# A transposed image in DRAM, laid out by row, place and tile column instead of by place, row and tile column

## The chip, the cores and the metric

The kernel runs on one core of one Trainium2 chip. The metric is the device time of one execution in microseconds. The kernel before takes 2478.38 us, the median of 3 runs (2473.84 to 2490.16). The execution that the profile shows has a span of 2488.3 us.

## The reference

The input x has 8 images of 256 channels and 56 x 56 pixels, in float32. Two layers follow each other, each with a residual.

```python
# layer 0: an involution: a 7x7 kernel per pixel and per group of 16 channels
def _L0_conv_ref(x, w_reduce, b_reduce, w_span, b_span):
    ker = jnp.einsum('bchw,oc->bohw', x, w_reduce) + b_reduce[None, :, None, None]
    ker = jnp.einsum('bchw,oc->bohw', ker, w_span) + b_span[None, :, None, None]
    ker = ker.reshape(B, G, 1, K * K, H, W)
    xp = jnp.pad(x, ((0, 0), (0, 0), (PAD, PAD), (PAD, PAD)))
    patches = jnp.stack([xp[:, :, i:i + H, j:j + W] for i in range(K) for j in range(K)], axis=2)
    patches = patches.reshape(B, G, C // G, K * K, H, W)
    return (ker * patches).sum(axis=3).reshape(B, C, H, W)

x = x + _L0_conv_ref(_gn(x), ...)
# layer 1: group norm, then twice: 3x3 convolution with ternary weights, batch norm over all 8
# images, relu (the second adds the output of the first before its relu)
x = x + _L1_conv_ref(_gn(x), ...)
```

Here G = 16, K = 7, and `_gn` is a group norm with 32 groups. Each image's group norm needs the whole image, and each batch norm needs all images.

## The kernel before

The program has four stages. **Start:** the first image is loaded, its norm is computed, its transposed copy is written to DRAM, and both convolution weights are made ternary (`quantize`). **Involution:** 8 images, each as 4 "quarters". A quarter is 64 channels, and the upper and the lower half of the image lie in the two halves of the 128 partitions (`h * CH`), so one half image is 28 rows. **Two convolutions**, with a pass over all images each. **The end:** norms, residual and the output. The change touches the first two stages alone.

The involution is done as matrix products over tiles of `PY` x `PX` = 3 x 8 pixels. Such a tile needs a patch of `QY` x `QX` = 9 x 14 = 126 input pixels. A half image has `TY` = 10 rows of tiles and `TX` = 7 tile columns. To use the 126 pixels of a patch as the contraction, the normalised image must lie with pixels in partitions and channels in the free dimension. So it is transposed and kept in DRAM in `xt_d`, twice (even and odd images), per quarter. A "place" is a column of the patch, 0 to 13. Each tile column has its own 14 places, so neighbouring tile columns hold 6 of the places double.

- `prep(b)` writes the transposed copy of image b. It works on strips of `SR` = 14 rows. For one strip, GpSimd normalises it into `xn` (one buffer, line 559). In a later step of the order, TensorE transposes `xn` in 8 pieces, one for each x within a tile (line 567), into a PSUM tile of the pool `ps_p` (3 buffers, shared with `generate`, `reduce` and `quantize`), ScalarE copies it to `stg` (line 570), and tasks are left for SyncE to store it: the strip at its own places, the same again for the columns that are places of the tile before and of the tile after, and the 3 rows that the other half of the image needs as its border. This makes 6 stores a strip, in pieces of 512 bytes and, for the border, 256 bytes. `transfer()` issues one task in each row step.
- `load_q` (line 599) loads the 126 patch rows of one row of tiles, 126 partitions with 3584 bytes each, 4 row steps ahead (`NQB`).
- `generate` makes the matrices of the next quarter in 14 units of 24 or 32 matmuls (line 629) whose results VectorE (638) and ScalarE (633) take out of PSUM with the bias added.
- `apply_row` does the 56 matmuls of one row of tiles (line 662); `pick_out` takes the wanted blocks by ScalarE (674) and VectorE (675), and GpSimd adds them to the image (678).
- `reduce` makes the next image's reduced channels (line 526), during the third quarter.

The main loop walks through 40 row steps for each image, r = 0 to 39, 10 in each quarter. `pin` makes the order of the text the order on every engine. In one row step stand: one store of the finished quarter or one load of the next image (`X_AT` says at which r), one `transfer()`, `apply_row`, one `load_q`, statistics, `pick_out`, up to two units of `generate` (`PER_ROW`), and one half step of `prep` where r is in `STRIP_AT`. A half step is either the GpSimd operation of a strip or its transposes with what follows, so a strip takes two half steps. The next image's strips begin at r = 23 and end at r = 6 of the next image itself.

In the start the first image's strips are all done in a row, with no `pin`: `prep(0)` stands in the text before `quantize(w1)`, whose sum over partitions is a matmul (line 203) that VectorE needs for the mean (line 205). All units of the first quarter and `quantize(w2)` follow, and the buffers of `load_q` lie where the memory of `quantize` was.

Of the kernel before, what the change touches and what calls it, by code (L numbers as in the profile page):

```python
# [7 lines left out]
F32 = mybir.dt.float32  # L8
F32R = mybir.dt.float32r
AF = mybir.ActivationFunctionType  # L10
ALU = mybir.AluOpType
# [4 lines left out]
P = 128  # L16
# [24 lines left out]
LEAD = (PX - 1) * QY + PY - 1  # L41
# [4 lines left out]
KX = TX + 1  # L46
HQ = TY * PY + K - 1
EX = HQ * KX
SR = HH // 2
NSP = SR * KX  # L50

# [24 lines left out]
def involution_tri_block_kernel(  # L76
# [17 lines left out]
    xt_d = [[dram.tile([QX * EX, P], F32, tag=f"xtd{i}_{c}", name=f"xtd{i}_{c}")  # L94
# [338 lines left out]
    with ExitStack() as ph1:  # L433
# [70 lines left out]
        xn = fixed([P, PX, SR, KX], "xn")  # L504
        nc.gpsimd.memset(xn, 0.0)
        zero = xn.rearrange("p j r k -> p (j r k)")

        for d in (d for ds in xt_d for d in ds):
            for r0, n in ((0, 5), (PAD + HH, 8)):
                e = P * 5  # L510
                nc.sync.dma_start(
                    bass.AP(d[:].tensor, d[:].offset + r0 * KX * P, [[EX * P, QX], [e, n], [1, e]]),
                    zero[:QX * n, :e])
# [27 lines left out]
        PLACES = ((PX - PAD, PX, 1), (0, PX, 0), (0, QX - PX - PAD, -1))  # L541

        def prep(b):
# [3 lines left out]
            for c in range(NCQ):  # L547
                d = xt_d[b % 2][c][:]

                def store(src, j0, j1, shift, row, o, d=d):  # L550

                    x0 = PAD + j0 - PX * shift
                    n, w = src.shape[0], src.shape[2]
                    nc.sync.dma_start(
                        bass.AP(d.tensor, d.offset + (x0 * EX + row * KX + shift) * P + o,
                                [[P, n], [EX * P, j1 - j0], [1, w]]), src[:, j0:j1])

                for s in range(2):
                    nc.gpsimd.tensor_scalar(  # L559
                        xn[:, :, :, :TX].rearrange("p j r k -> p r k j"),  # L560
                        xs[b, c][:, s * SR * W:(s + 1) * SR * W].rearrange(
                            "p (r k j) -> p r k j", k=TX, j=PX),
                        prm[b][:, c, 0:1], prm[b][:, c, 1:2], ALU.mult, ALU.add)
                    yield
                    pt = ps_flat(f"pt_{b}_{c}_{s}")
                    for j in range(PX):
                        nc.tensor.transpose(pt[:NSP, j * P:(j + 1) * P],  # L567
                                            xn[:, j].rearrange("p r k -> p (r k)"), ident_sb)
                    stg = work.tile([P, PX, P], F32, tag="stg", name=f"stg_{b}_{c}_{s}")
                    nc.scalar.copy(stg[:NSP].rearrange("p j c -> p (j c)"), pt[:NSP])  # L570
                    before, own, after = PLACES

                    e = PAD * KX
                    border = (stg[:e, :, CH:], PAD + HH, 0) if s == 0 else \
                        (stg[NSP - e:NSP, :, :CH], 0, CH)
                    whole = (stg[:NSP], PAD + s * SR, 0)
                    for part in (((whole, own),), ((whole, before), (whole, after)),
                                 ((border, own), (border, before), (border, after))):
                        def run(part=part, store=store):
                            for (src, row, o), pl in part:  # L580
                                store(src, *pl, row, o)
                        tasks.append(run)
                    yield
# [9 lines left out]
        def load_q(b, c, ty):  # L593
# [3 lines left out]
            src = bass.AP(d.tensor, d.offset + PY * ty * KX * P,  # L597
                          [[EX * P, QX], [KX * P, QY], [1, TX * P]])
# [9 lines left out]
        def generate(b, c, a):  # L608
# [4 lines left out]
            for u in range(NU):  # L613
# [6 lines left out]
                for j in order:  # L620
                    py, px = (p0 + j) // PX, (p0 + j) % PX
                    o = LEAD - px * QY - py
# [134 lines left out]
        X_AT = (0, 1, 4, 5, 6, 7, 8, 9)  # L757
# [150 lines left out]
```

## Time and profile before

| | us |
|---|---|
| median of 3 runs | 2478.38 |
| span of the profile | 2488.3 |
| TensorE matmul busy | 1785.1 (72%) |
| TensorE weight load busy | 1672.5 (67%) |
| VectorE busy | 1665.6 (67%) |
| ScalarE busy | 1126.5 (45%) |
| GpSimd busy | 286.9 (12%) |

The stages can be told by the slices of the profile: about 191 us for the start, then 1154 us for the involution (about 147 us for each image), then about 895 us for the two convolutions and 248 us for the end. In the involution the DMA engines are busy for 79% of the time and move 220 GB/s; in the convolutions they are busy for about a third of it. The busy share of an engine says little here by itself, as every stage has another limit; what ends the idle time of TensorE in the involution is what has to be read.

### The profile page before, as it was taken

To read this page: it belongs to the slowest core of one execution; us is meant where nothing else is said; L and a number is where in the kernel's file an instruction comes from. 1 tells how busy PE (TensorE), PEld (TensorE's weight loads), DVE (VectorE), ACT (ScalarE), POOL (GpSimd) and SP (SyncE) were. 2 spreads that over 40 slices of the span, in tenths; PEclk is the share of its full clock that TensorE was granted. 3 is DMA by queue.
4 is the path that set the end of the run, shared out by engine and by line. 5 is a ranking of instruction groups with operands and counts; after the bars stand their busy time and mean duration, and the time that the engine had idled before them with its cause. 6 is when DMAs were issued, how large, how long until landed. Compare 5 with 4: busy or idle time off the path is not lost.

```text
span 2488.3 us, 68764 instructions
## 1 busy us (share of the span) xinstructions
PE 1785.1 (72%) x30120; PEld 1672.5 (67%) x30120; DVE 1665.6 (67%) x2554; ACT 1126.5 (45%) x2020; POOL 286.9 (12%) x427
## 2 busy tenths in 40 slices
PE   1416877878786887868775999999499999990000
PEld 1306766767675776767665999999499999990000
DVE  4475656464555646556556999999599999974444
ACT  0202433434343343434433667667356767754443
POOL 0101221212122121222211000000000000000000
PEclk9657988989899898989997999999799999995555
DMA  6538696887869687796866233232423323329998
GB/s 170 162 124 220 190 250 196 235 236 204 241 181 255 194 243 202 213 249 171 247 182 223 106 129 135 106 132 106 181 81 132 133 106 127 138 73 424 429 428 377
DMA packets 216199, 493.15 MB, mean 198 GB/s; under 512 B 38446, under 2 KB 139180, under 8 KB 207196
## 3 DMA queue, kind: packets, MB, share of 16 engines
q1 hardware_dynamic: 209584, 447.66, 56.6%
q10 hardware_dynamic: 6316, 41.09, 4.1%
q8 instruction: 237, 3.88, 0.6%
q14 instruction: 62, 0.51, 0.1%
HBM read 315.88 MB, written 172.81 MB: 196 GB/s over the span
## 4 chain that ended last, share of the span: by engine, by line
PE 64%; DMA 14%; issue 10%; DVE 7%; POOL 2%; ACT 2%; ACTq 0%; SPq 0%; POOLq 0%; DVEq 0%
PE c L386 34%; PE pg L629 15%; PE pa L662 8%; DMA y1f<-y1d 4%; PE pt L567 3%; PE pk L526 3%; DMA out_y<-x1f 3%; DMA q<-xtd 2%; POOL xn L559 2%; DVE a L638 2%; DMA w_w<-in_w 1%; DVE x1f L848 1%; DMA x1f<-x1d 1%; DMA y2f<-y2d 1%; ACT a L633 1%
## 5 line engine op out<-in xcount | busy, mean ns | idle before, releaser
L386 PE MATMUL c<-pl,wq 128*128 128x392 f32 x4608 | 857.1, 348 | 50.6 <-ACT pl L292 32.5
L386 PEld LDWEIGHTS c<-pl,wq 128*128 128x128 f32 x4608 | 855.2, 189 | 52.3 <-ACT pl L292 33.2
L638 DVE TENSOR_TENSOR a<-pg,bt 126x756 f32<-126x756 f32 (+3 forms) x640 | 393.5, 656 | 288.5 <-ACT a L633 255.9
L629 PE MATMUL pg<-kr,wl 64*126 64x140 f32 (+1 forms) x6144 | 493.5, 308 | 64.7 <-issue 39.6
L629 PEld LDWEIGHTS pg<-kr,wl 64*126 64x126 f32 x6144 | 428.5, 210 | 86.8 <-issue 61.5
L662 PE MATMUL pa<-a,q 126*32 126x48 f32 x17920 | 294.9, 215 | 220.5 <-issue 140.8
L662 PEld LDWEIGHTS pa<-a,q 126*32 126x32 f32 x17920 | 240.8, 117 | 279.1 <-issue 224.6
L633 ACT ACTIVATE a<-pg,bt 126x126 f32<-126x126 f32 x768 | 243.6, 475 | 235.6 <-PE pg L629 235.4
L674 ACT ACTIVATE inv<-pa,half_sb 128x168 f32<-128x168 f32 x320 | 125.8, 393 | 428.4 <-PE pa L662 418.7
L675 DVE SCALAR_TENSOR_TENSOR inv<-pa,half_sb,inv 128x168 f32<-128x168 f32 x320 | 117.9, 368 | 231.1 <-ACT inv L674 230.5
L678 POOL TENSOR_TENSOR x<-x,inv 128x168 f32<-128x168 f32 x320 | 165.8, 518 | 909.5 <-DVE inv L675 874.5
L292 ACT CAST pl<-r 128x812 fp32r<-128x812 f32 x192 | 162.4, 867 | 153.4 <-DVE r L287 136.4
L349 ACT ACTIVATE dummy<-y,nc 128x1568 f32<-128x1568 f32 x128 | 205.4, 1605 | 15.6 <-DVE y L372 14.3
L293 DVE TENSOR_TENSOR pl<-r,pl 128x812 fp32r<-128x812 f32 x192 | 186.5, 997 | 30.6 <-ACT pl L292 29.7
L137 DVE BATCH_NORM_STATS2 st<-x 128x6 f32<-128x392 f32 x256 | 137.6, 555 | 16.9 <-DMA x<-in_x 16.3
L829 ACT ACTIVATE xp<-raw,bi_bn,sc_bn 128x392 f32<-128x392 f32 (+1 forms) x128 | 84.8, 720 | 71.7 <-DVE a L287 57.1
L559 POOL TENSOR_SCALAR xn<-x,gn 128x784 f32<-128x784 f32 x64 | 108.6, 1696 | 28.1 <-PE pt L567 21.3
L819 ACT ACTIVATE xp<-raw,gn 128x392 f32<-128x392 f32 (+1 forms) x128 | 85.2, 721 | 56.7 <-DVE a L287 50.9
L567 PE MATMUL pt<-ident_sb,xn 128*112 128x128 f32 x512 | 79.9, 306 | 29.1 <-POOL xn L559 23.4
L273 POOL MEMSET xp<- 128x116 f32 x32 | 6.3, 197 | 818.5 <-DVE a L287 818.3
L846 DVE SCALAR_TENSOR_TENSOR y1f<-y2f,sc_bn,y1f 128x3136 f32<-128x3136 f32 x16 | 55.8, 3485 | 63.9 <-DMA y2f<-y2d 63.9
L570 ACT COPY stg<-pt 112x1024 f32<-112x1024 f32 x64 | 65.5, 1023 | 71.7 <-PE pt L567 46.4
(127 smaller groups left out, 1362.6 us busy)
## 6 DMA issues: line engine op xcount, KB each, us to landing
q<-xtd SPq DMA_DIRECT2D x320, 441.0 KB
xtd<-stg SPq DMA_DIRECT2D x64, 448.0 KB
raw<-x1d SPq DMA_DIRECT2D x32, 812.0 KB
raw<-y1d SPq DMA_DIRECT2D x32, 812.0 KB
x<-in_x SPq DMA_DIRECT2D x64, 392.0 KB
x1d<-x SPq DMA_DIRECT2D x64, 392.0 KB
y1d<-y SPq DMA_DIRECT2D x32, 784.0 KB
y2d<-y SPq DMA_DIRECT2D x32, 784.0 KB
```

Source lines behind the costliest of these rows:

```text
L137: nc.vector.bn_stats(st[:, j, :], xt[:, j * NC:(j + 1) * NC])
L292: nc.scalar.copy(hi, r)
L293: nc.vector.tensor_tensor(lo, r, hi.bitcast(F32), ALU.subtract)
L349: nc.scalar.activation(dummy, y[:, to], f, bias=shift[:, to:to + 1], accum_out=stats[:, to, j, n:n + 1])
L386: nc.tensor.matmul(ps[:, to, :NM], wq[:, k, t, dx, to * P:(to + 1) * P], part[:, t, :, dx:dx + W], start=(c == 0), stop=(c == last))
L559: nc.gpsimd.tensor_scalar(xn[:, :, :, :TX].rearrange("p j r k -> p r k j"), xs[b, c][:, s * SR * W:(s + 1) * SR * W].rearrange("p (r k j) ...
L567: nc.tensor.transpose(pt[:NSP, j * P:(j + 1) * P], xn[:, j].rearrange("p r k -> p (r k)"), ident_sb)
L629: nc.tensor.matmul(dst, wl[rows, c, gp, o:o + NQ], kr[py][rows, px, :], start=True, stop=True)
L633: nc.scalar.activation(whole[:, g0 + i, p0 + j], ps[:NQ, i, j * nt:(j + 1) * nt], AF.Identity, bias=bt[:, c, g0 + i, p0 + j:p0 + j + 1])
L638: nc.vector.tensor_tensor(dst[:, g0:g0 + 2, p0:p0 + nv].rearrange("q g p t -> q g t p"), ps[:NQ, :, t0 * nv:t1 * nv].rearrange("q i (t p) ...
L662: nc.tensor.matmul(ps[o:o + 32, k * 2 * n:(k + 1) * 2 * n], q[:NQ, k, o:o + 32], av[:, t + k, g * 2 * n:(g + 1) * 2 * n], start=True, stop ...
L678: nc.gpsimd.tensor_tensor(xv, xv, iv.rearrange("p t (y x) -> p y t x", x=PX), ALU.add)
```

## The change

The transposed image gets another order: row of the image, then place, then tile column, then channel. One row of the image at one place is then `RP` = 7 x 128 numbers, 3584 bytes in one piece, and the 126 patch rows of a row of tiles lie one behind the other, 451,584 bytes in all. To store in this order, the spreading to 14 places is done before the transpose: GpSimd writes each strip to `xn` by tile column, row and place, with three operations (the tile's own 8 columns, 3 from the tile before, 3 from the tile after). One tile column of a strip then has rows x 14 columns for one transpose, and [...] a strip has 7 rows (98 columns) instead of 14, with 7 transposes. ScalarE copies 98 x 896 numbers, and the strip is stored by one DMA. The first and the last strip of each quarter leave a second one, for the border. There are 4 strips a quarter instead of 2.

The half steps of `prep` are taken in every row step from r = 23 on until they run out, and `transfer` issues up to two tasks in a row step. The loads of the next image move to r = 0, 1, 4, 5, 7, 8, 10, 11. The patch's order becomes row first, so the weights' line `w_line` and the bias tile `b_tile` are laid out anew on the host; the matmuls on them keep their shapes.

```diff
-LEAD = (PX - 1) * QY + PY - 1
+LEAD = (PY - 1) * QX + PX - 1
-KX = TX + 1
 HQ = TY * PY + K - 1
-EX = HQ * KX
-SR = HH // 2
-NSP = SR * KX
+RP = TX * P
+SR = HH // 4
+NSP = SR * QX
...
-    xt_d = [[dram.tile([QX * EX, P], F32, tag=f"xtd{i}_{c}", name=f"xtd{i}_{c}")
+    xt_d = [[dram.tile([HQ * QX, RP], F32, tag=f"xtd{i}_{c}", name=f"xtd{i}_{c}")
...
-        xn = fixed([P, PX, SR, KX], "xn")
+        xn = fixed([P, TX, SR, QX], "xn")
...
-        PLACES = ((PX - PAD, PX, 1), (0, PX, 0), (0, QX - PX - PAD, -1))
+        PLACES = ((PAD, 0, PX), (0, PX - PAD, PAD), (PAD + PX, 0, PAD))
...
                     nc.sync.dma_start(
-                        bass.AP(d.tensor, d.offset + (x0 * EX + row * KX + shift) * P + o,
-                                [[P, n], [EX * P, j1 - j0], [1, w]]), src[:, j0:j1])
-
-                for s in range(2):
-                    nc.gpsimd.tensor_scalar(
-                        xn[:, :, :, :TX].rearrange("p j r k -> p r k j"),
-                        xs[b, c][:, s * SR * W:(s + 1) * SR * W].rearrange(
-                            "p (r k j) -> p r k j", k=TX, j=PX),
-                        prm[b][:, c, 0:1], prm[b][:, c, 1:2], ALU.mult, ALU.add)
+                        bass.AP(d.tensor, d.offset + row * QX * RP + (o or 0), [[RP, n]] + to), src)
+
+                for s in range(HH // SR):
+                    xv = xs[b, c][:, s * SR * W:(s + 1) * SR * W].rearrange(
+                        "p (r k j) -> p k r j", k=TX, j=PX)
+                    for k, (x0, j0, n) in enumerate(PLACES):
+                        to, fr = ((slice(0, TX), slice(0, TX)), (slice(1, TX), slice(0, TX - 1)),
+                                  (slice(0, TX - 1), slice(1, TX)))[k]
+                        nc.gpsimd.tensor_scalar(
+                            xn[:, to, :, x0:x0 + n], xv[:, fr, :, j0:j0 + n],
+                            prm[b][:, c, 0:1], prm[b][:, c, 1:2], ALU.mult, ALU.add)
                     yield
                     pt = ps_flat(f"pt_{b}_{c}_{s}")
-                    for j in range(PX):
-                        nc.tensor.transpose(pt[:NSP, j * P:(j + 1) * P],
-                                            xn[:, j].rearrange("p r k -> p (r k)"), ident_sb)
-                    stg = work.tile([P, PX, P], F32, tag="stg", name=f"stg_{b}_{c}_{s}")
-                    nc.scalar.copy(stg[:NSP].rearrange("p j c -> p (j c)"), pt[:NSP])
...
-                    for part in (((whole, own),), ((whole, before), (whole, after)),
-                                 ((border, own), (border, before), (border, after))):
-                        def run(part=part, store=store):
-                            for (src, row, o), pl in part:
-                                store(src, *pl, row, o)
-                        tasks.append(run)
+                    for k in range(TX):
+                        nc.tensor.transpose(pt[:NSP, k * P:(k + 1) * P],
+                                            xn[:, k].rearrange("p r x -> p (r x)"), ident_sb)
+                    stg = work.tile([P, TX, P], F32, tag="stg", name=f"stg_{b}_{c}_{s}")
+                    nc.scalar.copy(stg[:NSP].rearrange("p k c -> p (k c)"), pt[:NSP, :RP])
+                    tasks.append(lambda stg=stg, s=s: store(stg[:NSP], PAD + s * SR))
+
+                    e = PAD * QX
+                    if s == 0:
+                        tasks.append(lambda stg=stg: store(stg[:e, :, CH:], PAD + HH, 0))
+                    elif s == HH // SR - 1:
+                        tasks.append(lambda stg=stg: store(stg[NSP - e:NSP, :, :CH], 0, CH))
                     yield
...
-            src = bass.AP(d.tensor, d.offset + PY * ty * KX * P,
-                          [[EX * P, QX], [KX * P, QY], [1, TX * P]])
+            src = bass.AP(d.tensor, d.offset + PY * ty * QX * RP, [[RP, NQ], [1, RP]])
...
-                    o = LEAD - px * QY - py
+                    o = LEAD - py * QX - px
...
-        X_AT = (0, 1, 4, 5, 6, 7, 8, 9)
-        STRIP_AT = (23, 24, 26, 27, 29, 30, 32, 33, 35, 36, 38, 39, 2, 3, 5, 6)
+        X_AT = (0, 1, 4, 5, 7, 8, 10, 11)
+        STRIPS_AT = 23
...
-                transfer()
+                transfer(2)
...
-                if r in STRIP_AT:
-                    if r == STRIP_AT[0] and more:
-                        strips = prep(b + 1)
-                    next(strips, None)
+                if more and r == STRIPS_AT:
+                    strips = prep(b + 1)
+                next(strips, None)
```

## The prediction

> **What bounds the kernel now.** I read the busy times by stage first, then TensorE's waits in the involution, then the DMA queues, then the chain of the start. In the fence of stages, columns after the window are its length, then busy us (instructions) of PE, PEld, DVE, ACT, POOL, then the granted clock, the DMA share and GB/s. The first four windows are the four quarters of the fourth image, then the first quarter of the first image, then the first quarter of the last.
>
> ```profile
> 623.00:662.00 39.00, 25.68 (x706) 22.46 (x697) 19.05 (x39) 13.14 (x35) 8.27 (x11) 0.90 1.01 262
> 662.00:693.00 31.00, 24.86 (x802) 21.79 (x793) 21.83 (x48) 11.49 (x37) 5.19 (x10) 0.84 0.70 205
> 693.00:735.00 42.00, 37.53 (x925) 33.24 (x929) 21.95 (x56) 17.59 (x46) 8.59 (x12) 0.92 0.59 167
> 735.00:768.00 33.00, 25.25 (x762) 21.99 (x749) 17.70 (x36) 14.31 (x39) 11.71 (x14) 1.00 0.87 249
> ...
> 196.00:229.00 33.00, 25.04 (x744) 22.60 (x748) 19.68 (x39) 11.08 (x33) 4.88 (x9) 0.81 0.90 221
> ...
> 1210.00:1240.00 30.00, 25.02 (x762) 21.97 (x754) 16.79 (x34) 13.80 (x36) 8.12 (x11) 0.93 0.82 241
> ```
>
> TensorE has the most work in every quarter, and the first quarter is longest for its work: 39 us for 25.7 busy, with the DMA engines full (1.01). The same quarter takes 33 us in the first image, which stores no strips then, and 30 us in the last, which loads no next image then. What TensorE waits for in the involution (191 to 1345 us) says how DMA costs time:
>
> ```profile
> PE pa L662 <- issue: 140.8, 79, 5.1
> PE pa L662 <- DMA q<-xtd: 62.3, 11, 51.8
> PE pg L629 <- issue: 39.6, 24, 5.0
> ...
> PE pt L567 <- POOL xn L559: 10.1, 13, 1.6
> PE pt L567 <- issue: 4.1, 2, 2.3
> ```
>
> The patch loads are hardly waited for: of 62.3 us, 51.8 are one wait at the start. The rest is "issue", 140.8 + 39.6 + 4.1 = 184.5 us, 23 us an image. Here is one, in TensorE's timeline, in the middle of a unit whose data were all there:
>
> ```profile
> 652.91 0.70 PE L629 MATMUL pg<-kr,wl 64*126 64x126 f32 x7
> 658.60 3.13 PE L629 MATMUL pg<-kr,wl 64*126 64x126 f32 x25 [4.99 <-issue]
> ```
>
> Such gaps come about 129 matmuls apart (with weight loads 258 instructions). The page's queue list has the matching transfers:
>
> ```profile
> q8 instruction: 237, 3.88, 0.6%
> ```
>
> 3.88 MB / 237 = 16.4 KB each, one per 60,240 / 237 = 254 matmuls and weight loads. So TensorE waits for its own instructions[...]. In the quarters of the fourth and fifth image the waits on issue add up to 13.3 and 11.0 us in the first (share 1.01 and 0.98), 5.3 and 8.3 in the second (0.70, 0.79), 0 and 0 in the third (0.59, 0.60), 7.6 and 1.6 in the fourth (0.87, 0.87); 7.7 us in the first image's first quarter (0.90) and 4.7 us in the last's (0.82). From 1.0 to 0.82 that is 12 to 4.7, about 4 us for a tenth of the DMA share.
>
> The start is another matter. Its chain from 60 to 100 us:
>
> ```profile
> 68.82 1.10 PE pt L567 x8
> ...
> 70.08 1.68 POOL xn L559
> ...
> 87.21 1.97 PE pt L567 x8
> ...
> 89.34 1.67 POOL xn L559
> ...
> 91.06 1.96 PE pt L567 x8
> 93.02 0.23 PE sum_w L203 x2
> 93.27 0.16 DVE mean_w L205
> ```
>
> GpSimd and TensorE take turns on the one buffer `xn`, strip by strip, and the mean of the first weights stands behind the last strip. From there the chain runs on through the weights to the first patch load at 191.3 us. A microsecond more here is one at the end.
>
> [...] eight transposes take 1.03 us right after dense work (65.91 us in the chain) and 1.96 in the idle start, where the granted clock is 0.59.
>
> **The change part by part.**
>
> *Stores.* From 68 to 98 us only strips are stored, and this is the queue; below it is a stretch (677 to 700) of little else than patch loads:
>
> ```profile
> q1 hardware_dynamic: 15692, 7.06, 84.9%
> ...
> q1 hardware_dynamic: 1335, 4.46, 64.1%
> ```
>
> 84.9% of 16 engines over 30 us is 407 engine-us for 8 strips, 51 each. The loads: 0.641 x 16 x 23 = 236 engine-us for some 1192 pieces of 3584 bytes, 198 ns each. In the convolutions, with rows of some 6 KB, 106.4 MB take 31.5% of 16 x 895 us, which is 23.6 bytes a ns and would make 152 ns of 3584 bytes. A new strip of 98 pieces thus costs 15 to 19 engine-us; I take 16. A border is 294 pieces of 256 bytes, 5 engine-us at 18 ns (the average of the old small pieces is 407 / 15692 = 26 ns; half the bytes, so less). For 14 rows: 2 x 16 + 5 = 37 instead of 51. Bytes fall too, but by little: 4 x 343 + 2 x 73.5 KB a quarter instead of 2 x 868.
>
> *Load of the DMA engines.* First quarter: 3 old strips (153) become 5 new ones with 3 borders (95), 58 less of 39 x 16 = 624, or 0.09; two image loads move on to the second quarter, 2 x 64 pieces of 6272 bytes at 0.27 us by the convolutions' rate, 34 more, or 0.05. From 1.0 to 0.86, so 5.6 us less. Fourth quarter: about 0.09 less, 2 us. Second quarter: 3 strips, a border and two image loads more, 87 of some 33 x 16, 0.16; by the slope that is 6 us, but its waits hardly follow the share (5.3 at 0.70, where the fourth's mean is 4.6 at 0.87), so I take 2.5 us more. Sum: 5.1 us less an image. The new layout of the patch loads I cost at nothing: the pieces stay 3584 bytes each, and the loads are not waited for.
>
> *Transposes.* 16 x 7 = 112 instead of 8 x 8 = 64 an image, 48 more. Eight take 1.02 us in the chain of the fourth image (0.128 each), and the busy time over the involution gives 65.95 / 448 = 0.147. So 6.1 to 7.1 us more, on the engine that sets the pace; 6.5 with the handing over. Row steps with transposes now always have two units ahead of them, so I add no wait for GpSimd.
>
> *Copies and GpSimd.* ScalarE: 16 x 0.9 instead of 8 x 1.02 us, 6 us an image; it is busy 57 of 147, and behind it queue `pick_out` and PSUM releases, for which TensorE hardly waits (`pg` waits for VectorE 1.1 us in the whole stage). GpSimd: 392 + 2 x 126 elements in three operations. Bounds: half of 1.70 us plus 126 elements at 2.13 ns (the slope of its addition, 304 ns for 56 and 542 for 168) is 1.4; with 185 ns of fixed cost for each, 1.9. I take 1.65: 26 instead of 13.6 us an image, of 147; hidden, as only the additions to the image queue behind it. SyncE issues 24 stores an image instead of 48. The layouts of weights and bias keep all shapes: nothing.
>
> *Start.* 16 turns instead of 8. A turn is now 1.67 + 1.96 + 0.22 of handing over; then 1.65 + 1.71 (seven eighths) + 0.21 = 3.57. Two turns at the full clock (2.77), 13 at 3.57, and a last 1.71: 53.7 us instead of 27.2 (65.84 to 93.02). So 26.5 us more, with no work beside it on the chain. Bounds by the GpSimd price: 22.5 to 30.5.
>
> *Sum.* The seven images after the first have their strips in the loop: 26.5 + 7 x (6.5 - 5.1) = 36.3; 2478.4 + 36.3 = 2515.
>
> **The rivals.** *The lighter DMA pays more.* If the first quarter falls to the last image's 4.7 us and the other quarters to almost nothing, 15 of 23 us go: 2478.4 + 26.5 + 7 x (6.5 - 15) = 2445. For it: the wait is steep near a full share. Against it: the second quarter, at 0.70, still waits for 5 us, and bytes hardly fall. *About even.* A relief of 9 us an image gives 26.5 - 17.5, so 2487; also reached if the weights' sum is placed ahead of the last strips. *A wait takes its place.* Twice as many turns through `xn`, `ps_p` and ScalarE: with 0.5 us at each of 16 strips and a relief of 3, 2478.4 + 26.5 + 7 x 11.5 = 2585. [...] Against it: 10.1 us for that wait in the stage now.
>
> **How the numbers follow.** The sum as worked out 0.36, the new wait 0.10: slower 0.46. About even 0.28. More relief 0.26, faster. The range from 2438 to 2560 leaves out the lower part of the relief case and the upper half of the wait case.
>
> **What would show it.** Right: the weights' sum about 26 us later, near 119 us; 16 turns of 3.4 to 3.8 us; 896 transposes; TensorE's issue waits of 23 us an image fallen to about 17; first quarter near 0.85 of the DMA share. Wrong: the start grows by under 15 us; issue waits under 10 us or over 23 us an image; TensorE waiting for GpSimd at the transposes by over 5 us an image.

## The result and the profile after

The changed kernel takes 2519.45 us, the median of 4 runs (2506.92 to 2523.16). Beside it the kernel before took 2479.51 us on the same chip, the median of 4 runs as well. The ratio is 1.0147, with a 95% interval from 1.0098 to 1.0196: slower by 24 to 49 us. The profiled executions have spans of 2517.8 and 2488.3 us, 29.5 us apart. That is 10 us less than the medians differ, because the profile of the kernel before is of the longest of its four runs (2490.16). What follows the last product of a patch takes 1165.6 us in the changed kernel and 1166.4 in the kernel before, so all of the difference lies in the start and in the involution.

The page of the changed kernel, parts 1, 3 and 5 (part 5: line, engine, operation, output and input, count, then busy us and mean ns of one, then the idle time before it and its releaser):

```profile
PE 1841.1 (73%) x30504; PEld 1709.0 (68%) x30504; DVE 1668.8 (66%) x2554; ACT 1173.1 (47%) x2084; POOL 380.1 (15%) x747
...
q1 hardware_dynamic: 117024, 440.03, 53.6%
...
q8 instruction: 240, 3.93, 0.7%
...
L565 POOL TENSOR_SCALAR xn<-x,gn 128x126 f32<-128x126 f32 (+1 forms) x384 | 204.1, 555 | 37.2 <-PE pt L571 30.6
L574 ACT COPY stg<-pt 98x896 f32<-98x896 f32 x128 | 116.9, 913 | 145.1 <-PE pt L571 90.5
L571 PE MATMUL pt<-ident_sb,xn 128*98 128x128 f32 x896 | 149.1, 309 | 34.0 <-POOL xn L565 23.1
```

The reader sees the parts of the change in counts: 896 transposes, 128 copies, 384 GpSimd operations (1.59 us for the three of a strip), and far fewer packets on the data queue, 117,024 where there were 209,584. The traffic was relieved as meant. The question is why that bought so little.

Stages of the changed kernel, in the same order and columns as in the prediction (four quarters of the fourth image, first quarter of the first image, first quarter of the last):

```profile
646.00:685.00 39.00, 29.91 (x800) 25.99 (x791) 20.16 (x42) 15.56 (x40) 12.94 (x25) 0.82 0.88 232
685.00:722.00 37.00, 26.69 (x812) 23.55 (x804) 23.79 (x50) 14.32 (x38) 9.80 (x19) 0.91 0.82 232
722.00:763.00 41.00, 37.96 (x926) 33.54 (x925) 20.28 (x52) 17.99 (x45) 9.86 (x19) 0.92 0.50 152
763.00:795.00 32.00, 26.82 (x779) 23.23 (x767) 17.84 (x35) 15.64 (x41) 12.89 (x25) 0.95 0.74 229
215.00:250.00 35.00, 25.17 (x754) 22.30 (x754) 18.09 (x37) 11.13 (x33) 4.86 (x9) 0.85 0.92 220
1241.00:1273.00 32.00, 26.49 (x786) 23.32 (x785) 17.48 (x36) 15.14 (x40) 12.93 (x25) 0.95 0.70 217
```

The DMA share in the first quarter fell from 1.01 to 0.88, and yet this quarter takes 39 us, as before: TensorE is busy 4.2 us longer in it, at a granted clock of 0.82 instead of 0.90, while its waits on issue (in the list of waits of that window) fell from 13.3 to 8.7 us. The second quarter took over the moved image loads (share 0.82 instead of 0.70), is 6 us longer, and its waits on issue rose from 5.3 to 8.4 us.

TensorE's waits in the involution of the changed kernel (190 to 1400 us; columns: total us, times, longest us):

```profile
PE pa L660 <- issue: 99.4, 62, 5.1
PE pg L627 <- issue: 65.4, 26, 5.4
PE pa L660 <- DMA q<-xtd: 52.9, 5, 50.8
...
PE pt L571 <- issue: 10.1, 6, 2.3
PE pt L571 <- POOL xn L565: 5.1, 9, 0.7
```

Waits on issue add up to 99.4 + 65.4 + 10.1 = 174.9 us, where they were 184.5: 1.4 us less for each of the seven images that have strips in the loop. Of the 52.9 us for patches, 50.8 are the one wait at the start. The wait of transposes for GpSimd, the rival's new wait, is 5.1 us in all.

TensorE's busy time in the loop, from the first to the last row of tiles, first of all instructions and then of the transposes alone; in each pair the kernel before comes first (columns as in the table of stages; the short lines have PE and PEld alone):

```profile
196.00:1322.00 1126.00, 880.33 (x25132) 776.87 (x25132) 624.19 (x1355) 436.02 (x1175) 257.53 (x374) 0.90 0.79 217
215.80:1352.00 1136.20, 920.93 (x25446) 806.29 (x25450) 627.37 (x1356) 476.55 (x1231) 338.77 (x654) 0.91 0.73 210
...
196.00:1322.00 1126.00, 65.95 (x448) 51.35 (x448) 0.90 0.79 217
215.80:1352.00 1136.20, 120.00 (x784) 88.09 (x784) 0.91 0.73 210
```

The transposes are busy 54.1 us longer, all matmuls together 40.6. TensorE's listed waits in the loop are 31.2 us shorter in sum: 9.6 on issue, 9.4 for patches, 5.0 for GpSimd, 7.2 for others. So the loop grows by far less than the transposes take, and waits on issue are less than a quarter of what makes up for them. What SyncE needs to issue a patch load fell as well (ns: shortest, median, longest; the kernel before first):

```profile
L599 SPq DMA_DIRECT2D q<-xtd x320: 781/804/2677, 191.3 to 1315.2; - x160
L597 SPq DMA_DIRECT2D q<-xtd x320: 307/318/2296, 212.0 to 1345.2; - x160
```

The chain of the start in the changed kernel, one turn and the end of the last (start us, us, what; several windows of the one view are put together):

```profile
86.35 1.76 PE pt L571 x6
...
88.28 0.09 POOL xn L565
88.37 0.34 issue
88.71 0.72 POOL xn L565
89.43 0.04 issue
89.48 1.76 PE pt L571 x6
...
111.71 1.96 PE pt L571 x7
113.68 0.23 PE sum_w L202 x2
...
199.40 12.29 DMA wqd<-u_w
212.01 3.26 DMA q<-xtd
```

A turn is 89.48 - 86.35 = 3.13 us. The sum of the weights comes at 113.68 instead of 93.02 us, 20.7 later. From there the chain runs through the same steps as before. The first patch load at its end is 1.1 us shorter (3.26 instead of 4.33), and the first product of a patch comes 19.6 us later. GpSimd's timeline has the three operations of the turn as

```profile
88.28 1.59 POOL L565 TENSOR_SCALAR xn<-x,gn 128x126 f32<-128x126 f32 x3 [1.53 <-PE pt L571]
```

The view of the tile `pa` gives this and the length of the loop (the two times are first and last start); first the kernel before, then the changed one:

```profile
L662 PE MATMUL pa<-a,q x17920: 176/206/291, 196.2 to 1321.9; 126*32 126x48 f32 x182, 126*32 126x16 f32 x18
```

```profile
L660 PE MATMUL pa<-a,q x17920: 176/206/290, 215.8 to 1352.2; 126*32 126x48 f32 x182, 126*32 126x16 f32 x18
```

The loop took 1321.9 - 196.2 = 1125.7 us and takes 1352.2 - 215.8 = 1136.4, 10.7 more. With 19.6 of the start that is 30.3, and 0.8 less behind the loop makes the difference of the spans. By the medians, which are 39.9 us apart, the loop's part is nearer 20 us. The start's part is the steadier one: the first product comes between 212.8 and 216.2 us in all eight kernels below that keep the start of the changed kernel, and between 196.2 and 196.7 in the three that keep the old one.

### The profile page after: what moved, and what is told of

It reads as the page before. It is cut to its first block, busy times and chain, and to the rows that moved or that the text cites. A ratio compares the mean times of both kernels' runs of the same rounds, so it can differ in the third digit from the quotient of the medians.

```text
span 2517.8 us, 69784 instructions
## 1 busy us (share of the span) xinstructions
PE 1841.1 (73%) x30504; PEld 1709.0 (68%) x30504; DVE 1668.8 (66%) x2554; ACT 1173.1 (47%) x2084; POOL 380.1 (15%) x747
## 3 DMA queue, kind: packets, MB, share of 16 engines
q1 hardware_dynamic: 117024, 440.03, 53.6%
## 4 chain that ended last, share of the span: by engine, by line
PE 65%; DMA 14%; issue 10%; DVE 7%; POOL 2%; ACT 1%; ACTq 0%; SPq 0%; POOLq 0%; DVEq 0%
PE c L385 34%; PE pg L627 15%; PE pa L660 8%; PE pt L571 5%; DMA y1f<-y1d 3%; DMA out_y<-x1f 3%; PE pk L524 3%; DMA x1f<-x1d 2%; DMA q<-xtd 2%; DVE a L636 2%; POOL xn L565 1%; DMA w_w<-in_w 1%; DVE x1f L845 1%; ACT a L631 1%; DMA y1d<-y 1%
## 5 line engine op out<-in xcount | busy, mean ns | idle before, releaser
L385 PEld LDWEIGHTS c<-pl,wq 128*128 128x128 f32 x4608 | 854.2, 189 | 53.3 <-ACT pl L291 33.1
L627 PE MATMUL pg<-kr,wl 64*126 64x140 f32 (+1 forms) x6144 | 492.0, 308 | 88.6 <-issue 65.4
L660 PE MATMUL pa<-a,q 126*32 126x48 f32 x17920 | 287.6, 213 | 164.3 <-issue 99.4
L565 POOL TENSOR_SCALAR xn<-x,gn 128x126 f32<-128x126 f32 (+1 forms) x384 | 204.1, 555 | 37.2 <-PE pt L571 30.6
L574 ACT COPY stg<-pt 98x896 f32<-98x896 f32 x128 | 116.9, 913 | 145.1 <-PE pt L571 90.5
L571 PE MATMUL pt<-ident_sb,xn 128*98 128x128 f32 x896 | 149.1, 309 | 34.0 <-POOL xn L565 23.1
L571 PEld LDWEIGHTS pt<-ident_sb,xn 128*98 128x98 f32 x896 | 106.3, 141 | 65.6 <-POOL xn L565 38.4
```

The costliest lines, as they stand in the source:

```text
L385: nc.tensor.matmul(ps[:, to, :NM], wq[:, k, t, dx, to * P:(to + 1) * P], part[:, t, :, dx:dx + W], start=(c == 0), stop=(c == last))
L565: nc.gpsimd.tensor_scalar(xn[:, to, :, x0:x0 + n], xv[:, fr, :, j0:j0 + n], prm[b][:, c, 0:1], prm[b][:, c, 1:2], ALU.mult, ALU.add)
L571: nc.tensor.transpose(pt[:NSP, k * P:(k + 1) * P], xn[:, k].rearrange("p r x -> p (r x)"), ident_sb)
L627: nc.tensor.matmul(dst, wl[rows, c, gp, o:o + NQ], kr[py][rows, px, :], start=True, stop=True)
L660: nc.tensor.matmul(ps[o:o + 32, k * 2 * n:(k + 1) * 2 * n], q[:NQ, k, o:o + 32], av[:, t + k, g * 2 * n:(g + 1) * 2 * n], start=True, stop ...
```

## The experiments

Open were three terms of the prediction: whether the start's microseconds count one for one, what a transpose costs the loop, and why a lighter DMA relieved the waits so little. Each run was compared with the kernel before on the same chip. The chips differ, so rows are compared by their ratios and not by their medians. "First row" is the first product of a patch and "loop" the time from it to the last one, both from the tile view of `pa`. "Issue" and "patch" are TensorE's waits in the loop on its own instructions and on the patch loads, all in us of one profile.

| kernel | median us | ratio [95%] | first row | loop | issue | patch |
|---|---|---|---|---|---|---|
| before | 2479.51 | 1 | 196.2 | 1125.7 | 184.5 | 62.3 |
| after | 2519.45 | 1.0147 [1.0098, 1.0196] | 215.8 | 1136.4 | 174.9 | 52.9 |
| a_start | 2523.17 | 1.0112 [1.0085, 1.0138] | 209.3 | 1134.0 | 178.1 | 42.2 |
| b_start | 2479.20 | 0.9946 [0.9925, 0.9968] | 187.5 | 1124.3 | 180.5 | 54.0 |
| b_late | 2478.96 | 0.9962 [0.9948, 0.9976] | 186.9 | 1132.9 | 175.2 | 34.0 |
| a_nostore | 2454.70 | 0.9841 [0.9799, 0.9882] | 215.3 | 1075.3 | 133.1 | 52.8 |
| b_nostore | 2448.14 | 0.9830 [0.9803, 0.9856] | 196.7 | 1082.7 | 163.6 | 52.4 |
| a_twice | 2568.28 | 1.0322 [1.0284, 1.0361] | 216.1 | 1183.3 | 145.8 | 55.7 |
| a_xat | 2528.43 | 1.0156 [1.0118, 1.0194] | 216.1 | 1147.3 | 177.0 | 58.0 |
| a_small | 2517.62 | 1.0133 [1.0097, 1.0169] | 214.9 | 1131.7 | 165.5 | 53.0 |
| b_xcut | 2531.77 | 1.0174 [1.0132, 1.0217] | 196.5 | 1158.2 | 100.2 | 171.5 |
| a_qsmall | 2533.93 | 1.0199 [1.0170, 1.0228] | 215.8 | 1149.4 | 149.5 | 70.5 |
| a_xeo | 2514.11 | 1.0114 [1.0087, 1.0142] | 212.8 | 1138.4 | 157.2 | 53.3 |
| a_96 | 2507.55 | 1.0093 [1.0067, 1.0118] | 216.2 | 1118.1 | 157.2 | 51.9 |

The loop of before, b_start and b_late holds the same work and scatters over 9 us; a difference of one loop below that says nothing by itself. Its parts scatter as much: waits on issue from 175.2 to 184.5 us, and TensorE's busy time from 880.2 us at a granted clock of 0.90 (before) to 891.3 and 891.4 at 0.89 (b_start, b_late). The fall of 9.6 us in the changed kernel's waits on issue is therefore hardly more than scatter. Names with a_ start from the changed kernel, those with b_ from the kernel before.

**The start: a_start, b_start and b_late.** The first image's strips are taken off the chain of the weights. The same move is made in both kernels:

```diff
-        for _ in prep(0):
-            transfer(len(tasks))
...
             quantize(wq_d[0], w1, ...)
+            for _ in prep(0):
+                transfer(len(tasks))
```

b_late has the two added lines behind the second `quantize` instead.

> The changed kernel, with the first image's strips moved in the text behind the first quantize, so that the sum of the weights on TensorE no longer stands behind them; nothing is left out. Theory A (the start's strips are on the chain one for one, in both kernels): the sum comes at about 66 us instead of 113.7, the first row of tiles at about 169 us instead of 215.8, and the time is 2519 - 47 = 2472 us. Rival (another chain of the start, the second weights or the strips themselves, takes over): the first row comes at 195 us or later and the time stays above 2495 us.

> The kernel before with the same move of the first image's strips. Theory A: the sum at about 66 us instead of 92.8, the first row of tiles at about 169 us instead of 196.2, time 2479 - 27 = 2452 us, and the two kernels with this move differ by the loop alone, about 20 us less than they differ without it. Rival: less than 10 us gained.

> The kernel before with the first image's strips moved in the text behind the second quantize, so that neither the sums on TensorE nor the load of the second weights on ScalarE's queue stand behind them; nothing is left out. Theory A2 (in the first move the strips' copies and store waits held up the load of the second weights on ScalarE's queue; without that the start's chain is that of the weights alone): sum at 66 us, load of the second weights issued at about 97 us, first row of tiles at 168 to 174 us instead of 196, time 2479 - 25 = 2454 us. Rival (the strips, now last and slowed on GpSimd by VectorE's work on the weights, become the end of the start): first row at 185 us or later, 2470 us or more.

In a_start the sum of the weights comes at 65.95 us, 47.7 earlier, but the first row only 6.5 earlier, and the timed ratio, 1.0112, can't be told from the changed kernel's. Its chain of the start (start us, us, what) shows what took over:

```profile
69.71 7.97 POOL xn L565 x3
...
80.59 10.48 POOL xn L565 x2
...
112.40 14.57 DMA xtd<-stg
127.07 0.91 ACT stg L574
128.36 7.31 DMA xtd<-stg
...
136.17 5.04 DMA w_w<-in_w
```

GpSimd's strip operations take 8.0 and 10.5 us on the chain, and then the strips' copies on ScalarE wait for stores to free `stg`. The loads of the second weights (`w_w`) are issued by ScalarE, behind these copies, and end after 141 us. GpSimd's timeline of the same run (start us, us, operation, and in brackets the idle time before it) sets a slow group beside a quick one:

```profile
79.20 11.86 POOL L565 TENSOR_SCALAR xn<-x,gn 128x126 f32<-128x126 f32 x3 [1.53 <-PE pt L571]
92.59 1.60 POOL L565 TENSOR_SCALAR xn<-x,gn 128x126 f32<-128x126 f32 x3 [1.53 <-PE pt L571]
```

The slow one runs while VectorE makes the first weights ternary (68 to 91 us in VectorE's timeline), the quick one just after: 1.60 us become 11.86. What holds GpSimd up there isn't shown.

b_start gains 8.7 us in the first row, of the 27 that its strips had taken. Its timed gain, 0.5%, makes it faster than both kernels. In it ScalarE issues the second weights' loads from 99.7 to 116.6 us, among the strips' copies and their waits for stores. b_late moved the strips out of ScalarE's way: these loads are issued from 97 to 104 us (from 123 us on in the kernel before). Yet its first row comes hardly earlier than b_start's, at 186.9 against 187.5 us. GpSimd's timeline of b_late:

```profile
136.68 0.38 POOL L200 PARTITION_ALL_REDUCE amx_w<-mx_w  x1 [6.29 <-issue]
...
144.38 4.61 POOL L559 TENSOR_SCALAR xn<-x,gn 128x784 f32<-128x784 f32 x1 [6.98 <-issue]
...
155.32 5.64 POOL L559 TENSOR_SCALAR xn<-x,gn 128x784 f32<-128x784 f32 x1 [2.19 <-PE pt L567]
```

The strips there stand behind the weights' own reduction on GpSimd, stretch again beside VectorE's work on the weights (4.61 and 5.64 us between 140 and 164 us, where one took 1.67 at 128.7 us), and the last stores leave SyncE only at 182 us. In all three runs, moving the strips off the chain of the first weights brought 6.5 to 9.3 us in the first row and no more: the moved strips, slower on GpSimd or in the way of the next loads, made another chain that close behind. A microsecond put on this chain counted nearly one for one (20.7 became 19.6), but one taken off it by moving the work did not.

**No strip stores: a_nostore and b_nostore.**

```diff
+                    if b > 0:
+                        yield
+                        continue
...
-            d = xt_d[b % 2][c][:]
+            d = xt_d[0][c][:]
```

> The changed kernel without the strip stores of images 1 to 7; every image loads the patches of image 0's copy, so the output of layer 0 is that of other patches for 7 images. All loads, transposes, copies and operations of GpSimd stay. Theory A (the stores of the changed kernel cost TensorE about 4 us of waiting for instructions an image): 2519 - 7 x 4 = 2491 us. Rival of the prediction (waits follow the DMA share at 4 us for a tenth in each loaded quarter): share falls by about 0.1, 8 to 12 us an image, 2435 to 2463 us. If the stores cost nothing: 2519 us.

> The kernel before without the strip stores of images 1 to 7, every image loading image 0's copy as above. Theory A (its stores cost about 5 us an image): 2479 - 35 = 2444 us, so that the two kernels without stores differ by 47 us: 20 of the start and 27 of the 48 more transposes an image. Rival of the prediction (waits follow the share, which falls by 0.17): 14 us an image or more, 2380 us or less, and a difference to the changed kernel without stores of 65 us, 6.5 us an image for the transposes.

TensorE's waits in the involution, without the old stores and then without the new ones:

```profile
PE pa L665 <- issue: 112.4, 67, 5.0
...
PE pg L632 <- issue: 48.5, 28, 4.3
```

```profile
PE pa L663 <- issue: 83.6, 55, 6.1
...
PE pg L630 <- issue: 48.9, 27, 5.4
```

In the loop, the stores cost 1125.7 - 1082.7 = 43.0 us in the kernel before and 1136.4 - 1075.3 = 61.1 in the changed one. By the timed ratios it is 1.7% and 3.06%, so 42 and 76 us; the difference, 34, has an uncertainty of 17 (intervals of the three other ratios, added in squares). So the new stores cost more time. The data queue in the loop windows had 77.3% of the 16 engines with the old stores and 64.6% without (1126 and 1082.5 us), 71.7% with the new ones and 63.9% without (1136 and 1075). That makes (0.773 x 16 x 1126 - 0.646 x 16 x 1082.5) / 7 = 391 engine-us an image (busy time summed over the 16 engines) for the old stores and, in the same way, 292 for the new. **The stores that use a quarter less of the DMA engines cost more time.** Their waits on issue are dearer too: 174.9 - 133.1 = 41.8 us against 184.5 - 163.6 = 20.9. The rest of the cost lies elsewhere. With the old stores, patches were waited for by 9.9 us more and TensorE was busy 11.5 us longer with the same matmuls (880.2 instead of 868.7). With the new ones patches cost nothing (0.1), and it was busy 20.0 us longer (921.1 instead of 901.1). The granted clock was 0.01 lower with stores in both pairs, 0.90 against 0.91 and 0.91 against 0.92; whether that is the reason wasn't tested.

Without stores the new loop is 7 us shorter than the old one, within the scatter, though it does 336 more transposes; it waits 30 us less on issue. By a_twice below the added transposes themselves account for some 12 of these. What gives the rest, about twice the scatter, is open: the patch layout, the moved image loads or the order of the strips; a_xat below undoes the loads alone.

**Transposes: a_twice.** Every transpose of images 1 to 7 is made twice, 784 more.

```diff
-                    for k in range(TX):
+                    for k in list(range(TX)) * (2 if b > 0 else 1):
```

> The changed kernel with every transpose of the strips of images 1 to 7 made twice, 784 more in all (112 an image); the second writes the same again. Theory A (a transpose costs TensorE's chain 0.13 us one for one): 2519 + 784 x 0.135 = 2625 us. Rival (transposes fall into time in which TensorE waits for its instructions, and more work between two fetches hides more of a fetch): at most half of it, 2570 us or less.

TensorE's waits on issue in a_twice:

```profile
PE pa L660 <- issue: 83.2, 50, 3.7
PE pg L627 <- issue: 58.9, 24, 5.4
```

The loop grew by 1183.3 - 1136.4 = 46.9 us, 0.060 us for each added transpose. The timed ratios give (1.0322 - 1.0147) x 2486.66 / 784 = 0.056, with an uncertainty of 0.020. The busy time of these operations grew by 208.6 - 120.0 = 88.6 us in the loop, 0.113 each, so about half of it cost no time. Against these 41.7 us stand 29.1 us by which the waits on issue became shorter, 0.037 for each added transpose, and about 15 us of busy time of the other matmuls, which fell from 801 to 786; why it fell isn't shown. In this loop, work put into an engine that waits for its instructions was about half free (41.7 of 88.6 us).

**Moved image loads: a_xat.** The old moments of the image loads, in the new layout.

```diff
-        X_AT = (0, 1, 4, 5, 7, 8, 10, 11)
+        X_AT = (0, 1, 4, 5, 6, 7, 8, 9)
```

> The changed kernel with the loads of the next image back at the row steps of the kernel before (0, 1, 4, 5, 6, 7, 8, 9). Rival of the prediction (moving two of them out of the first quarter relieved it by about 2 us an image net): 2519 + 10 to 15 = 2529 to 2534 us. Theory A (the waits go where the loads go): no change, 2512 to 2526 us.

No difference that the runs can tell: 1.0156 against 1.0147, where the two intervals together leave some 15 us open. The moved loads are neither a gain nor a loss that can be seen.

**Length of pieces: a_small, b_xcut, a_qsmall and a_xeo.** These test a guess of the author, that long packets ahead of an instruction fetch make it late. a_small writes each strip as two DMAs in pieces of 512 bytes, instead of one in pieces of 3584:

```diff
-                        src, to = src.rearrange("p k c -> p (k c)"), [[1, RP]]
+                        for k0 in range(2):
+                            nc.sync.dma_start(
+                                bass.AP(d.tensor, d.offset + row * QX * RP + k0 * P,
+                                        [[RP, n], [2 * P, len(range(k0, TX, 2))], [1, P]]),
+                                src[:, k0::2])
+                        return
```

> The changed kernel with each strip's store cut into 512-byte pieces again, by two DMAs over the even and the odd tile columns; same bytes, same places, all other work the same. Theory A [...]: DMA share up by about 0.03, waits on issue no longer or shorter, 2505 to 2519 us. Rival of the prediction (waits follow the DMA share alone): 2530 to 2545 us.

1.0133 against 1.0147: no difference beyond some 15 us. So there is no sign that the length of the stores' pieces is what makes them dear.

b_xcut, in the kernel before, makes each image load and each store of the layer's output four DMAs in pieces of 1568 instead of 6272 bytes; a_xeo does it in the changed kernel with two DMAs; a_qsmall does what a_small does, for the patch loads.

```diff
-            nc.sync.dma_start(xs[b, c][h * CH:(h + 1) * CH],
-                              x[b, c * CH:(c + 1) * CH, h * NHW:(h + 1) * NHW])
+            m = NHW // 4
+            for i in range(4):
+                nc.sync.dma_start(xs[b, c][h * CH:(h + 1) * CH, i * m:(i + 1) * m],
+                                  x[b, c * CH:(c + 1) * CH, h * NHW + i * m:h * NHW + (i + 1) * m])
...
```

> The kernel before with each load of the next image and each store of a finished quarter cut into four DMAs of 1568-byte pieces instead of one of 6272-byte pieces; same bytes. Theory A (a fetch of instructions waits the longer, the longer the packets of the other queue are): the waits on issue fall from 23 us an image by 3 to 6, 2430 to 2455 us. Rival of the prediction (waits follow the share, which rises a little): 2479 to 2495 us.

TensorE's waits in b_xcut:

```profile
PE pa L664 <- DMA q<-xtd: 171.5, 58, 51.9
PE pa L664 <- issue: 78.0, 58, 3.1
...
PE pg L631 <- issue: 22.2, 18, 2.5
```

Waits on issue fell from 184.5 to 100.2 us, and the longest from 5.1 to 3.1. But the patches came late, 171.5 us of waits instead of 62.3, and the kernel got slower. SyncE issues 48 more DMAs an image; whether that or the DMA engines made the patches late wasn't separated.

```diff
-            nc.sync.dma_start(q[:NQ].rearrange("p k c -> p (k c)"), src)
+            for k0 in range(2):
+                src = bass.AP(d.tensor, d.offset + PY * ty * QX * RP + k0 * P,
+                              [[RP, NQ], [2 * P, len(range(k0, TX, 2))], [1, P]])
+                nc.sync.dma_start(q[:NQ, k0::2], src)
```

> The changed kernel with each patch load made by two DMAs, over the even and the odd tile columns, in 512-byte pieces instead of 3584-byte ones; same bytes, nothing left out. Theory A ([...] in the kernel before with its image loads and stores cut to 1568 bytes, issue waits fell from 184.5 to about 100 us): the waits on issue fall from 175 us to 120 or less, time 2455 to 2480 us, if the second issue on SyncE doesn't make the patches late. Rival (the share alone counts): waits on issue 165 to 185 us, time 2510 to 2530 us.

The same trade at a smaller size: 25.4 us less on issue, 17.6 more on patches (35 waits instead of 5), and the queue's share of the loop up from 71.7% to 82.3%. The loop is 13 us longer than in the changed kernel; in the timed runs the intervals overlap (1.0170 to 1.0228 and 1.0098 to 1.0196), so it is no faster, and slower not for certain.

```diff
...
+            for e in range(2):
+                to, fr = (v.rearrange("p (n e m) -> p n e m", n=2, e=2)[:, :, e] for v in (
+                    xs[b, c][h * CH:(h + 1) * CH],
+                    x[b, c * CH:(c + 1) * CH, h * NHW:(h + 1) * NHW]))
+                nc.sync.dma_start(to, fr)
...
```

> The changed kernel with each image load and each store of a finished quarter made by two DMAs over the even and the odd fourths of a row, in 1568-byte pieces; 16 more issues on SyncE an image instead of the 48 more of the four-way cut. Theory A (length of packets): waits on issue fall to 100 to 130 us, and with a SyncE queue that keeps up the patches are not late, 2450 to 2480 us. Rival (share alone, or the patches come late whatever the number of issues): 2515 us or more.

Issue waits fell by 17.7 us with patch waits unchanged, but the loop did not become shorter (1138.4), and 1.0114 overlaps the changed kernel's interval. The trace shows what took the place of the waits: TensorE was busy for 940.8 us with the same matmuls instead of 921.1, at a granted clock of 0.88 in the loop instead of 0.91. This profile has the lowest clock of the kernel's four runs (0.860, the others 0.868 to 0.874), so its loop can't show what the pieces are worth. With shorter pieces the waits on issue were lower in all four kernels, by 9 to 84 us (the 9 of a_small is within the scatter); no time that the runs can tell came of it.

**Rows of a store: a_96.** Each store of 98 rows becomes one of 96 and one of 2. The bytes stay the same; the run asks whether the number of rows has a part in what a store costs.

```diff
...
-                        bass.AP(d.tensor, d.offset + row * QX * RP + (o or 0), [[RP, n]] + to), src)
+                        bass.AP(d.tensor, d.offset + (row * QX + past) * RP + (o or 0), [[RP, n]] + to), src)
...
-                    tasks.append(lambda stg=stg, s=s: store(stg[:NSP], PAD + s * SR))
+                    def run(stg=stg, s=s, store=store):
+                        store(stg[:96], PAD + s * SR)
+                        store(stg[96:NSP], PAD + s * SR, past=96)
+                    tasks.append(run)
```

> The changed kernel with each strip's store cut into one of 96 rows and one of 2 rows[...]. Theory B (the new stores cost more than the old [...]): the stores' cost falls from 61 us in the loop towards 45, time 2500 to 2507 us. Theory A (packet length): no change, 2512 to 2525 us.

TensorE's waits on issue in a_96:

```profile
PE pa L663 <- issue: 92.3, 51, 4.8
PE pg L630 <- issue: 55.3, 26, 5.8
...
PE pt L571 <- issue: 9.6, 7, 2.7
```

The loop is 18.3 us shorter than in the changed kernel, and the stores' cost in it is back at 1118.1 - 1075.3 = 42.8 us, the old value. Issue waits fell by 17.7.

No row of a trace names the DMA engine of a packet, so how a store is spread over the engines isn't shown. But each packet is in the trace with its start and its duration, so the packets in flight at one time can be counted. Between 60 and 125 us, where the first image's strips are stored, the count of the stores' 3584-byte packets is most often 14 in the changed kernel (for 10.3 us; 16 for 0.2) and most often 16 in a_96 (for 7.6 us; 14 for 1.3). Short packets spread the count more (those of 512 bytes up to 23 in the kernel before, those of 3584 up to 17 in the changed one), so they are compared by themselves: with packets of 512 bytes it is most often 16 in the kernel before (for 4.7 us; 14 for 2.4), whose strips have 112 rows, and 14 in a_small, whose strips have 98. The patch loads of 126 rows most often have 14 in flight too (for 4.0 us in the kernel before, up to 200 us; 16 for 0.2). Beside a_nostore, the stores of the changed kernel raise the part of the loop with 13 or 14 packets in flight from 27.1% to 33.3%, and that with 15 or more only from 30.5% to 33.2%. Those of a_96 leave the first as it is, at 26.6%, and raise the second to 40.2%.

That the number of packets in flight is behind what the stores cost in time is likely but not settled: the timed intervals, up to 1.0118 and from 1.0098, still overlap.

## Why the prediction was right, and where its terms were off

The forecast, 2515 us, is 4.5 below the measured 2519.45, and the case worked out as the likeliest is the one that came. The start carries it, and there the mechanism was right. In the loop the sum holds better than its terms, and that was luck.

- **Start: right in mechanism, the term mis-sized.** 26.5 us forecast, 19.6 measured. The sum of the weights moved by 20.7 us instead of 26.5, outside the forecast of "near 119", and below the bounds that were given (22.5 to 30.5). The turn was taken as 3.57 us, to lie between 3.4 and 3.8, and is 3.13. The working added all of GpSimd's 1.65 us; its three operations do take 1.59, but the chain holds only 0.09 + 0.34 + 0.72 = 1.15 of it. The rest lies beside the next transposes. In the turn that is shown they end at 89.87, 0.39 us after the transposes have started at 89.48: an outer tile column has a neighbour on one side only, so two of the three operations complete it, and its transpose need not wait for the third. (The lower bound for GpSimd, 1.4 us, comes out with both pieces of 126 elements, not with the one that its sentence names.)
- **Transposes: mis-sized.** 6.5 us an image forecast. The busy time did come, 54.1 us or 7.7 an image, but a transpose added in a_twice cost the loop 0.060 us, which makes 48 x 0.060 = 2.9. The step took busy time as time of the end. TensorE waits for instructions some 23 us an image, and part of the new work filled that.
- **Relief of the waits on issue: this step failed.** The loads came as forecast: the stores fell from 391 to 292 engine-us an image, where the working has 8 x 51 = 408 and 8 x 37 = 296, and the first, second and fourth quarter have shares of 0.88, 0.82 and 0.74. The slope, "about 4 us for a tenth of the DMA share", did not hold: 1.4 us an image came instead of 5.1. Even this is no relief by a lighter DMA: at the 0.037 us of a_twice, 48 added transposes shorten the waits by 1.8 us an image by themselves. The pairs without stores show that the share is the wrong measure. Old stores raise it by 12.7 points and bring 20.9 us of issue waits; new ones raise it by 7.8 and bring 41.8.
- **The sum of the loop: luck.** Forecast 7 x (6.5 - 5.1) = 9.8 us; measured 10.7 in the two profiles and nearer 20 by the medians. Both terms were too large, by some 3.6 us an image each, and these errors cancelled. The 2.9 and the 1.4 don't make a new sum, as the 2.9 already holds the waits that the transposes fill; at 2.9 and no relief the loop grows by 7 x 2.9 = 20 us, which the timed runs allow.
- **Copies and GpSimd at nothing: right.** Transposes wait 5.1 us for GpSimd in the whole stage, less than the 10.1 of before, though it has twice as many turns. The rival of a new wait falls with that.
- **SyncE and the layout of the patch loads at nothing: a small gain was missed, the rest is open.** One patch load now occupies SyncE for 318 instead of 804 ns (median of 320), and the patch waits after the first fell from 10.5 to 2.1 us. Without the old stores they are 0.4 us in the old layout too, so the fewer stores may be enough for this. Without stores the new loop waits 30 us less on issue than the old one, of which the transposes explain some 12, and a_xat shows no part of the rest in the moved loads. Whether it is the patch layout or the spread of the strips wasn't tried.
- **The rivals with more relief** needed the lighter DMA to pay 9 to 15 us an image. The waits on issue fell by 1.4.

## What to carry to other kernels

A lower DMA share is not yet time: ask which wait it shortens, and measure what a stream costs by taking it out, since here the lighter stores were the dearer ones. Cost work added to an engine that waits for its own instructions at less than its busy time (here 0.060 us for 0.113 busy), and measure that by doubling it. Work put on the chain of a start counts nearly one for one (here 19.6 us of 20.7), while moving work off it pays only down to the next chain, here 6.5 to 9 us behind; look for that one in the queues of the engines that issue the loads and at what the moved work will run beside. Before a store's rows are chosen, count the packets that it keeps in flight: with 98 rows there were most often 14, with 96 and 112 rows 16. And when a wait gets shorter but the time doesn't, look at the busy time of the same work and at the granted clock.

## What the runs showed of the hardware

- GpSimd beside VectorE's work on the weights: three operations on a strip took 1.60 us just after it and 7.96 and 11.86 beside it (a_start); one took 1.67 us at 128.7 us and 1.96 to 5.64 between 144 and 166 us, beside it (b_late). Of VectorE's operations with results of 1536 elements that take 1.75 us with GpSimd idle (before, 99 to 117 us), most took 1.74 to 1.76 there, single ones up to 2.95.
- TensorE's waits for its own instructions were 184.5 us in the loop before and 163.6 without the strip stores (b_nostore), 174.9 us in the changed loop and 133.1 without them (a_nostore), 145.8 with every transpose made twice (a_twice), and 100.2 us in the loop before with image loads and stores in pieces of 1568 bytes (b_xcut). TensorE went on 1.45 us after the end of the last transfer of instructions (median of 85 waits in the kernel before; the middle eight tenths lie between 1.27 and 1.59).
- Pieces of 512 bytes in the stores cost no time over pieces of 3584 that the runs can tell (a_small: 1.0133 against 1.0147), while in the patch loads they raised the queue's share from 71.7% to 82.3% of the loop (a_qsmall).
- Stores of 98 rows most often had 14 packets in flight, stores of 96 or 112 rows 16 (98: after, 14 for 10.3 us and 16 for 0.2, and a_small; 96: a_96, 16 for 7.6 us and 14 for 1.3; 112: before, 16 for 4.7 us and 14 for 2.4; at 60 to 125 us).
- Issuing a patch load of 126 x 3584 bytes took SyncE 804 ns where the source had three dimensions and 318 ns where it had two (before, after).
